# Two graph layers on one core: layer 1's values and residual taken from rows by VectorE instead of from transposes by TensorE and ScalarE

## The chip, the cores and the metric

The kernel runs on one core of a Trainium2 chip. A core has TensorE (matrix products, written to PSUM), VectorE and ScalarE (elementwise work on PSUM and SBUF), GpSimd, and DMA queues. The metric is the device time of one execution in microseconds, the median of several runs. The profile is of one execution.

## The reference

The input is x (16 batches of 1024 rows of 256 numbers, float32) and adj (16 x 1024 x 1024, zeros and ones, about 3% ones).

Layer 0 is graph attention with 4 heads of 64. With one edge type present its logit is a source term plus a destination term, through a leaky ReLU, masked by adj:

```
h = einsum('bnd,hde->bhne', x, W)
weight = leaky_relu(mask * (e_src[i] + e_dst[j]), 0.01)      # -1e9 where adj is 0
out = relu(softmax(weight) @ h + bias) + h
out = (out - mean) / sqrt(var + 1e-6) * ln_gamma + ln_beta   # over the 64 of each head
x = layernorm(x + heads side by side)                        # over 256
```

Layer 1 is attention with 8 heads of 32, in which queries, keys and values are one and the same tensor, and then an MLP:

```
normed = layer_norm(x, gamma1, beta1)
out = softmax(normed @ normed.T / sqrt(32), masked by adj) @ normed
x1 = x + out
y = layer_norm(x1, gamma2, beta2)
mlp = gelu(y @ W1 + b1) @ W2 + b2                            # 256 -> 1024 -> 256
x = layernorm(x + x1 + mlp)
```

All products are float32.

## The kernel before

**Tiles.** A batch's 1024 rows are 8 blocks of 128; four blocks make a half of 512. Two streams of steps, `layer0` and `layer1`, run over the batches; layer 0 of the next batch is interleaved with layer 1 of the present one. All instructions are issued through one recording helper, so the profile gives every one the line L61 and groups are told apart by tile names.

**Layer 0** (`prepare`, line 471; `attention0`, 541). A batch's rows are turned (`xT`), multiplied with the weights (`acc<-w0e,xT`), and the adjacency rows are turned by TensorE and made into a mask by ScalarE (`mask`). The softmax weights of layer 0 are made by VectorE (`p<-cb,dinv,mask`), and 16 steps per batch multiply them with the values (`acc<-v,p`). When one head of one half is done, `residual0` (line 616) takes the reciprocal of the sums, divides and applies ReLU, and adds the result to `hb`. Before the change the middle part is four ScalarE activations, one for each block of 128 rows, scaled by that row's reciprocal. `after0` (626) then norms each head, adds the input, takes the statistics of the 256, and makes

- `normed` (tile `sq`): the rows after both norms, which ScalarE computes from `hb`;
- `nT`: these rows turned by TensorE (`transpose_rows`, 376), with gamma1 and beta1 applied by ScalarE as it copies them from PSUM, where they are numbers per partition. These are layer 1's queries and keys;
- `v1` (tile `v`): the values, with a column of ones. Before the change `nT` is turned back by TensorE, eight 128x128 transposes for a half, into two PSUM tiles, and copied by ScalarE;
- `x1`: the residual, `normed` times a ratio per row, by ScalarE. `ratio` undoes the second norm's scale.

**Layer 1** (`attention1`, 710). 32 steps per batch. A step makes logits for four heads (`ps<-nT`, four PSUM tiles), exponentials by ScalarE (`p<-ps`), the mask by VectorE (`p<-p,mask`), and, three steps later (`LAG`), the weighted products (`po<-p,v`, `po<-p,unit`, `po<-v,p`). `finish1` (816) adds x1, norms and turns; it also adds the attention result to x1, and `add_bias2` (837) adds the row b2. The MLP (`mlp`, 848) has TensorE groups `ps<-yT,w_sb` and `po<-w_sb,hid` with ScalarE's gelu between; `last_norm` (907) adds x1, norms and writes a block out (tile `z`).

**PSUM.** Two banks `acc` serve layer 0 and the transposes while layer 1 is in its attention (`bank0`, 357); a bank is taken when the chain that reads it has been issued. While the MLP runs, transposes use the four `ps` banks (`side_bank`, 370). So the turning back of `nT` shows as `acc<-ident,nT` and as `ps<-ident,nT`.

**What sets the order.** Each engine runs its instructions in the order of the program, and the program is written by a planner. `Pace` (line 90) keeps a modelled time for each engine: `enter` (143) gives each instruction a start and an end from modelled costs. `chains` holds the side work (residuals, norms, transposes) as generators; each `yield` names the engine of what follows and the tiles that it needs, and `advance` (433) lets those go on whose needs are met in the model. The main loop (line 997) takes the next step from `layer0` or `layer1` by comparing layer 0's progress with a wanted course: `COURSE` (982) says how far layer 0 is to be when layer 1 has done so much of its batch. The model's times exist only while the program is written; on the chip the engines wait for each other by semaphores.

Of the kernel before, what the change touches and what calls it, by code (L numbers as in the profile page):

```python
# [31 lines left out]
F32 = mybir.dt.float32  # L32
# [4 lines left out]
OP = mybir.AluOpType  # L37
PSUM = bass.MemoryType.PSUM

P = 128  # L40
# [49 lines left out]
class Pace:  # L90
# [5 lines left out]
    def __init__(self, nc):  # L96
        self.nc = nc
        self.free = dict.fromkeys(self.LATENCY, 0.0)
        self.written, self.read = {}, {}
        self.array = self.table = self.last = None  # L100

        self.born = self.settle = lambda tile: None
        for name in self.LATENCY:
            setattr(self, name, Engine(self, name))
# [38 lines left out]
    def enter(self, engine, op, args, kwargs):  # L143
        aps = [a for a in (*args, *kwargs.values()) if isinstance(a, bass.AP)]
        out, ins = aps[0].tensor.name, [a.tensor.name for a in aps[1:]]
        if op == "dma_start":
            start = max(self.now(), self.through(out))
            self.written[out] = start + self.LATENCY["sync"]
            return
        start = max(  # L150
            [self.free[engine], self.read.get(out, 0.0)] + [self.written.get(i, 0.0) for i in ins if i != out]
        )
        end = self.free[engine] = start + self.cost(engine, op, aps, args[2] if len(args) > 2 else None)
        self.written[out] = max(self.written.get(out, 0.0), end + self.LATENCY[engine])
        if "accum_out" in kwargs:
            out = kwargs["accum_out"].tensor.name
            self.written[out] = max(self.written.get(out, 0.0), end + self.LATENCY[engine])
        for i in ins:
            self.read[i] = max(self.read.get(i, 0.0), end)
# [3 lines left out]
def fast_path(  # L163
# [120 lines left out]
    for i, (_, _, dst) in enumerate(terms):  # L284
# [8 lines left out]
                )  # L293
            nc.vector.tensor_reduce(dst[:, c, :], t, axis=mybir.AxisListType.X, op=OP.add)

    lng0_r, lnb0_r, b2_r = [
        const.tile([P, D], F32, name=name) for name in ("lng0_r", "lnb0_r", "b2_r")
    ]
    g1_c, be1_c, g2_c, be2_c = [const.tile([P, DC], F32, name=name) for name in ("g1_c", "be1_c", "g2_c", "be2_c")]
    w1_sb = const.tile([P, DC, DFF], F32, name="w1_sb")  # L300
# [3 lines left out]
    def at_time(t):  # L304
        return lambda: t

    def later_weights():
        for t, src in ((lng0_r, lng0), (lnb0_r, lnb0), (b2_r, b2)):
            nc.sync.dma_start(t, bass.AP(tensor=src.tensor, offset=src.offset, ap=[[0, P], [1, D]]))
        for t, src in ((g1_c, gamma1), (be1_c, beta1), (g2_c, gamma2), (be2_c, beta2)):  # L310
            nc.sync.dma_start(t, src.rearrange("(c p) -> p c", p=P))
        nc.sync.dma_start(b1_sb, b1.rearrange("c p -> p c"))
        yield "tensor", at_time(nc.now() + 6.0)
        nc.sync.dma_start(w1_sb, w1.rearrange("(c p) f -> p c f", p=P))
        nc.sync.dma_start(w2_sb, w2.rearrange("(c p) d -> p c d", p=P))
        yield "tensor", at_time(nc.now() + 24.0)

        pb = ps_o.tile([P, FC], F32, name="po")
        for f in range(FC):
            for c in range(DC):  # L320
                nc.tensor.matmul(
                    pb[:, f : f + 1],
                    w1_sb[:, c, f * P : (f + 1) * P],
                    be2_c[:, c : c + 1],
                    start=c == 0,
                    stop=c == DC - 1,
                )
        yield "vector", pb
        nc.vector.tensor_add(b1_sb, b1_sb, pb)
        for c in range(DC):  # L330
            nc.vector.tensor_scalar(w1_sb[:, c, :], w1_sb[:, c, :], g2_c[:, c : c + 1], None, op0=OP.mult)
# [283 lines left out]

    def residual0(av, h, rinv):

        t = two.tile([P, BPH, HO], F32, name="relu")
        nc.vector.reciprocal(rinv, av[:, :, HO])
        yield "scalar", rinv  # L620
        for q in range(BPH):
            nc.scalar.activation(t[:, q, :], av[:, q, 0:HO], AF.Relu, scale=rinv[:, q : q + 1])
        yield "vector", t
        nc.vector.tensor_add(h, h, t)

    def after0(b, n, hd, o):


        for first in range(hd + 1):
            complete(residuals[b, n, first])  # L630
        rowwise = [P, BPH, D]
        heads = slice((hd - PAIR + 1) * HO, (hd + 1) * HO)
        oh = o[:, :, heads].rearrange("p g (h e) -> p g h e", e=HO)
        per_head = [P, BPH, PAIR, HO]
        s = small.tile([P, BPH, PAIR], F32, name="s0")
        nc.vector.tensor_reduce(s, oh, axis=mybir.AxisListType.X, op=OP.add)
        nc.vector.scalar_tensor_tensor(
            oh, s[:, :, :, None].to_broadcast(per_head), -1.0 / HO, oh, op0=OP.mult, op1=OP.add
        )
        yield "scalar", o  # L640
        sq = two.tile([P, BPH, PAIR * HO], F32, name="oT1")
        nc.scalar.activation(sq, o[:, :, heads], AF.Square)
        if hd == H0 - 1:
            xl = one.tile(rowwise, F32, name="xl")
            load_x(xl, b, n * BPH, BPH)
        yield "vector", sq
        v = small.tile([P, BPH, PAIR], F32, name="v0s")
        nc.vector.tensor_reduce(
            v, sq.rearrange("p g (h e) -> p g h e", e=HO), axis=mybir.AxisListType.X, op=OP.add
        )  # L650
        nc.vector.tensor_scalar(v, v, 1.0 / HO, EPS_HEAD, op0=OP.mult, op1=OP.add)
        r = power(v.rearrange("p g e -> p (g e)"), BPH * PAIR, "r0").rearrange("p (g e) -> p g e", e=PAIR)
        pair = o[:, :, heads]
        nc.vector.tensor_mul(pair, pair, lng0_r[:, None, heads].to_broadcast([P, BPH, PAIR * HO]))
        if hd == H0 - 1:
            nc.vector.tensor_add(xl, xl, lnb0_r[:, None, :].to_broadcast(rowwise))
        yield "vector", r
        nc.vector.tensor_mul(oh, oh, r[:, :, :, None].to_broadcast(per_head))
        if hd < H0 - 1:
            return  # L660
        complete(norms[b, n, PAIR - 1])
        nc.vector.tensor_add(o, o, xl)
        yield "vector", o
        mv = small.tile([P, BPH, 2], F32, name="mv0")
        for g in range(BPH):
            statistics(o[:, g, :], mv[:, g, :])

        v2 = small.tile([P, 2, BPH], F32, name="v2")  # L670
        nc.vector.tensor_scalar(v2[:, 0, :], mv[:, :, 1], 1.0 + EPS, EPS * EPS, op0=OP.mult, op1=OP.add)
        r2 = power(v2[:, 0, :], BPH, "r2")
        nc.vector.tensor_scalar(v2[:, 1, :], mv[:, :, 1], EPS, None, op0=OP.add)
        r3 = power(v2[:, 1, :], BPH, "r3")
        yield "vector", r2
        t = minus_mean(mv[:, :, 0], r2, BPH)
        yield "scalar", t
        normed = one.tile(rowwise, F32, name="sq")
        scale_shift(normed, o, t, r2, BPH)
        yield "tensor", normed, side_ready  # L680
        nT = two.tile([P, DC, HALF], F32, name="nT")
        for g in range(0, BPH, GB):
            transpose_rows(nT[:, :, g * P : (g + GB) * P], normed[:, g : g + GB, :], g1_c, be1_c)
            yield "tensor", normed, side_ready
        yield "tensor", nT, side_ready
        v1 = two.tile([P, BPH, H1, HD + 1], F32, name="v1")
        nc.vector.memset(v1[:, :, :, HD], 1.0)
        for g in range(0, BPH, GB):
            pt = side_bank([P, GB, DC, P])
            for i in range(GB):  # L690
                for c in range(DC):
                    nc.tensor.transpose(pt[:, i, c, :], nT[:, c, (g + i) * P : (g + i + 1) * P], ident)
            nc.scalar.copy(
                v1[:, g : g + GB, :, 0:HD], pt.rearrange("p g c (h e) -> p g (c h) e", e=HD)
            )
            yield "tensor", nT, side_ready
        handed[b, n] = [None, v1, nT]
        yield "vector", r3

        ratio = small.tile([P, BPH], F32, name="ratio")  # L700
        nc.vector.tensor_mul(ratio, v2[:, 0, :], r2)
        nc.vector.tensor_mul(ratio, ratio, r3)
        yield "scalar", ratio
        x1 = three.tile(rowwise, F32, name="x1")
        for g in range(BPH):
            nc.scalar.mul(x1[:, g, :], normed[:, g, :], ratio[:, g : g + 1])
        handed[b, n][0] = x1


# [195 lines left out]
            yield 1.75, before_ready  # L905

    def last_norm(b, k, po, x1):
        z = four.tile([P, 1, D], F32, name="z")
        nc.vector.tensor_add(z[:, 0, :], po, x1)
        mv = small.tile([P, 2], F32, name="mv")  # L910
        statistics(z[:, 0, :], mv)
# [67 lines left out]
    ATTN1 = 2.0 + 2.5 * (NH * NB * H1 // QUAD)  # L979
    WORK1 = ATTN1 + NB // GB * (1.75 * FC / 2 + 3.5 * GB)  # L980
    SLACK = 0.06
    COURSE = [(0.0, 1.0), (ATTN1, 1.40), (WORK1 - 10.0, 2.0), (WORK1, 2.0)]

    def wanted():
        b, done = place[1]
# [475 lines left out]
```

## Time and profile before

| | before |
|---|---|
| time, median of 3 (lowest to highest) | 3663.35 us (3662.82 to 3672.89) |
| span of the profiled execution | 3665.6 us |
| mean granted TensorE clock | 0.976 |
| TensorE busy | 3506.3 us |
| VectorE busy | 2840.2 us |
| ScalarE busy | 2191.5 us |
| GpSimd busy | 428.7 us |

From the second batch on, a batch repeats after 223.8 to 223.9 us. A row of the groups gives engine and operation, output tile and inputs, their shapes, the count, then the busy time of the group and the mean length of one instruction in ns, then the idle time of that engine in front of them and what ended it. A row of the waits gives the engine and the tile it was about to write, the engine and tile it waited for, the total in us, how often, and the longest.

### The profile page before, as it was taken

To read this page: it belongs to the slowest core of one execution; us is meant where nothing else is said; L and a number is where in the kernel's file an instruction comes from. 1 tells how busy PE (TensorE), PEld (TensorE's weight loads), DVE (VectorE), ACT (ScalarE), POOL (GpSimd) and SP (SyncE) were. 2 spreads that over 40 slices of the span, in tenths; PEclk is the share of its full clock that TensorE was granted. 3 is DMA by queue.
4 is the path that set the end of the run, shared out by engine and by line. 5 is a ranking of instruction groups with operands and counts; after the bars stand their busy time and mean duration, and the time that the engine had idled before them with its cause. 6 is when DMAs were issued, how large, how long until landed. Compare 5 with 4: busy or idle time off the path is not lost.

```text
span 3665.6 us, 142190 instructions
## 1 busy us (share of the span) xinstructions
PE 3506.3 (96%) x64673; PEld 2368.4 (65%) x64673; DVE 2840.2 (77%) x4882; ACT 2191.5 (60%) x5024; POOL 428.7 (12%) x424
## 2 busy tenths in 40 slices
PE   6899999999999999999999999999999999999998
PEld 4567575675856658576585766757567585665846
DVE  5787787878878787787887868778787887878784
ACT  2665746557475574746647466574755747557474
POOL 0102011010110101101020110201101011010100
PEclk9899999999999999999999999999999999999999
DMA  4111101011010110201101011110101102010000
GB/s 102 33 18 33 29 14 37 15 37 24 15 41 11 36 23 16 45 6 40 20 27 34 13 35 17 33 29 14 39 14 35 26 14 43 11 36 9 16 6 14
DMA packets 77525, 97.30 MB, mean 27 GB/s; under 512 B 9072, under 2 KB 59760, under 8 KB 76912
## 3 DMA queue, kind: packets, MB, share of 16 engines
q0 software_dynamic: 18432, 33.56, 6.1%
q1 hardware_dynamic: 56896, 53.50, 4.6%
q8 instruction: 508, 8.32, 0.9%
q10 hardware_dynamic: 1584, 1.05, 0.1%
q14 instruction: 105, 0.86, 0.1%
HBM read 104.87 MB, written 16.78 MB: 33 GB/s over the span
## 4 chain that ended last, share of the span: by engine, by line
PE 87%; ACT 8%; DVE 3%; issue 1%; DMA 0%; ACTq 0%; POOL 0%; POOLq 0%; DVEq 0%
PE ps L61 33%; PE po L61 33%; PE acc L61 21%; ACT p L61 3%; DVE p L61 2%; ACT mask L61 1%; ACT sq L61 1%; ACT nT L61 1%; ACT v L61 0%; ACT relu L61 0%; DMA w0e<-in_L_gnn_W_dram 0%; ACT z L61 0%; ACT cb L61 0%; DVE z L61 0%; ACT oT L61 0%
## 5 line engine op out<-in xcount | busy, mean ns | idle before, releaser
L61 ACT ACTIVATE p<-ps 128x512 f32<-128x512 f32 x2048 | 1061.8, 617 | 402.1 <-PE ps L61 402.1
L61 DVE TENSOR_TENSOR p<-p,mask 128x1024 f32<-128x1024 f32 x1024 | 1187.9, 1218 | 103.0 <-ACT p L61 101.3
L61 PE MATMUL ps<-nT 32*128 32x512 f32 x4096 | 795.4, 654 | 11.0 <-ACT cb L61 9.8
L61 DVE SCALAR_TENSOR_TENSOR p<-cb,dinv,mask 128x512 f32<-128x512 f32 x1024 | 698.9, 744 | 28.6 <-ACT cb L61 28.6
L61 PEld LDWEIGHTS po<-v,p 128*32 128x32 f32 x32768 | 401.1, 111 | 323.5 <-issue 279.7
L61 PE MATMUL acc<-v,p 128*64 128x65 f32 x16384 | 546.2, 225 | 28.6 <-ACT relu L61 13.2
L61 PEld LDWEIGHTS acc<-v,p 128*64 128x64 f32 x16384 | 507.4, 139 | 96.1 <-issue 47.4
L61 PE MATMUL po<-p,v 128*32 128x512 f32 x2048 | 559.1, 621 | 0.0
L61 PE MATMUL po<-p,unit 128*32 128x512 f32 x2048 | 558.5, 621 | 0.0
L61 ACT ACTIVATE hid<-ps,b_sb 128x256 f32<-128x256 f32 x512 | 241.4, 476 | 437.1 <-PE ps L61 435.0
L61 PE MATMUL ps<-yT,w_sb 128*128 128x256 f32 x2048 | 480.0, 384 | 0.0
L61 PE MATMUL po<-w_sb,hid 128*128 128x256 f32 x2048 | 477.0, 384 | 0.0
L61 PEld LDWEIGHTS po<-w_sb,hid 128*128 128x128 f32 x2048 | 382.4, 190 | 74.5 <-issue 22.7
L61 PEld LDWEIGHTS ps<-yT,w_sb 128*128 128x128 f32 x2048 | 379.8, 190 | 51.8
L61 PE MATMUL po<-v,p 128*32 128x33 f32 x32768 | 392.5, 199 | 4.6 <-issue 4.5
L61 PEld LDWEIGHTS ps<-nT 32*128 32x128 f32 x4096 | 284.9, 187 | 153.2 <-ACT p L61 52.0
L61 PEld LDWEIGHTS po<-p,v 128*32 128x32 f32 x2048 | 79.4, 109 | 339.9 <-DVE p L61 171.9
L61 POOL TENSOR_TENSOR r<-v,mhalf 128x1 f32<-128x1 f32 (+1 forms) x192 | 168.0, 880 | 574.7 <-DVE v L61 540.1
L61 DVE TENSOR_TENSOR z<-acc,bias_r 128x256 f32<-128x256 f32 x128 | 54.2, 423 | 219.5 <-ACT hb L61 217.8
L61 POOL TENSOR_TENSOR r<-v1s,mhalf 128x4 f32<-128x4 f32 x32 | 61.9, 1934 | 1214.9 <-DVE v1s L61 1214.9
L61 POOL TENSOR_TENSOR r<-v0s,mhalf 128x8 f32<-128x8 f32 x64 | 128.9, 2014 | 522.6 <-DVE v0s L61 522.6
L61 POOL DMA_DIRECT2D ak<-in_adj_dram x128 | 69.8, 545 | 914.3 <-PE acc L61 903.9
(113 smaller groups left out, 3078.8 us busy)
## 6 DMA issues: line engine op xcount, KB each, us to landing
ak<-in_adj_dram POOLq DMA_DIRECT2D x128, 256.0 KB, 4.0
xk<-in_x_dram SPq DMA_DIRECT2D x64, 256.0 KB, 3.4
xl<-in_x_dram SPq DMA_DIRECT2D x32, 512.0 KB, 4.0
out_dram<-z SPq DMA_DIRECT2D x128, 128.0 KB, 1.7
w_sb<-in_L_gnn_W_dram SPq DMA_DIRECT2D x2, 1024.0 KB, 6.6
v<-in_L_gnn_a_src_dram SPq DMA_DIRECT2D x2, 320.0 KB, 4.9
v<-in_L_gnn_a_dst_dram ACTq DMA_DIRECT2D x1, 320.0 KB, 7.0
xl<-in_L_gnn_a_dst_dram ACTq DMA_DIRECT2D x1, 320.0 KB, 6.2
```

Of the source, the lines that this page charges most:

```text
L61: return method(*args, **kwargs)
```

## The change

Layer 1's values are `normed` times gamma1 as a row, computed by VectorE, so that nothing is turned back. Beta1 is left out of the values: the attention weights of a row sum to one, so that it adds beta1 to every output, and it goes into x1 instead, which VectorE makes in one instruction (times ratio, plus the row). Because x1 is added twice on the way to the output, b2 is made b2 - beta1 once at the start. ReLU and division of layer 0 become one VectorE product per head and half, max(av, 0) times the reciprocal. In the planner, TensorE's costs are doubled for a while behind a modelled wait of over 1.5 us[...]; the course's middle point goes from 1.40 to 1.42. The ReLU tile has one buffer instead of two, and `z` three instead of four, which makes room for two rows of constants.

```diff
@@ Pace.enter
-        end = self.free[engine] = start + self.cost(engine, op, aps, args[2] if len(args) > 2 else None)
+        cost = self.cost(engine, op, aps, args[2] if len(args) > 2 else None)
+        if engine == "tensor":
+            if start > self.free[engine] + 1.5:
+                self.slow = start + 3.0
+            if start < self.slow:
+                cost *= 2.0
+        end = self.free[engine] = start + cost
@@ later_weights
-        for t, src in ((lng0_r, lng0), (lnb0_r, lnb0), (b2_r, b2)):
+        for t, src in ((lng0_r, lng0), (lnb0_r, lnb0), (g1_r, gamma1), (be1_r, beta1), (b2_r, b2)):
...
+        nc.vector.tensor_sub(b2_r, b2_r, be1_r)
@@ residual0
-        t = two.tile([P, BPH, HO], F32, name="relu")
+        t = one.tile([P, BPH, HO], F32, name="relu")
         nc.vector.reciprocal(rinv, av[:, :, HO])
-        yield "scalar", rinv
-        for q in range(BPH):
-            nc.scalar.activation(t[:, q, :], av[:, q, 0:HO], AF.Relu, scale=rinv[:, q : q + 1])
-        yield "vector", t
+        nc.vector.scalar_tensor_tensor(
+            t, av[:, :, 0:HO], 0.0, rinv[:, :, None].to_broadcast([P, BPH, HO]), op0=OP.max, op1=OP.mult
+        )
         nc.vector.tensor_add(h, h, t)
+        yield from ()
@@ after0
-        yield "tensor", nT, side_ready
+        yield "vector", normed
         v1 = two.tile([P, BPH, H1, HD + 1], F32, name="v1")
         nc.vector.memset(v1[:, :, :, HD], 1.0)
-        for g in range(0, BPH, GB):
-            pt = side_bank([P, GB, DC, P])
-            for i in range(GB):
-                for c in range(DC):
-                    nc.tensor.transpose(pt[:, i, c, :], nT[:, c, (g + i) * P : (g + i + 1) * P], ident)
-            nc.scalar.copy(
-                v1[:, g : g + GB, :, 0:HD], pt.rearrange("p g c (h e) -> p g (c h) e", e=HD)
+        for g in range(BPH):
+            nc.vector.tensor_mul(
+                v1[:, g, :, 0:HD],
+                normed[:, g, :].rearrange("p (h e) -> p h e", e=HD),
+                g1_r.rearrange("p (h e) -> p h e", e=HD),
             )
-            yield "tensor", nT, side_ready
...
-        yield "scalar", ratio
+        yield "vector", ratio, at_time(nc.now() + 12.0)
+
         x1 = three.tile(rowwise, F32, name="x1")
         for g in range(BPH):
-            nc.scalar.mul(x1[:, g, :], normed[:, g, :], ratio[:, g : g + 1])
+            nc.vector.scalar_tensor_tensor(
+                x1[:, g, :], normed[:, g, :], ratio[:, g : g + 1], be1_r, op0=OP.mult, op1=OP.add
+            )
@@ last_norm
-        z = four.tile([P, 1, D], F32, name="z")
+        z = three.tile([P, 1, D], F32, name="z")
@@ the course
-    COURSE = [(0.0, 1.0), (ATTN1, 1.40), (WORK1 - 10.0, 2.0), (WORK1, 2.0)]
+    COURSE = [(0.0, 1.0), (ATTN1, 1.42), (WORK1 - 10.0, 2.0), (WORK1, 2.0)]
```

More of the change, by code (lines that the diff above doesn't have):

```diff
@@ L100, in __init__ @@
         self.array = self.table = self.last = None
+        self.slow = 0.0
         self.born = self.settle = lambda tile: None
@@ L294, in fast_path @@
             nc.vector.tensor_reduce(dst[:, c, :], t, axis=mybir.AxisListType.X, op=OP.add)
-    lng0_r, lnb0_r, b2_r = [
-        const.tile([P, D], F32, name=name) for name in ("lng0_r", "lnb0_r", "b2_r")
+    lng0_r, lnb0_r, g1_r, be1_r, b2_r = [
+        const.tile([P, D], F32, name=name) for name in ("lng0_r", "lnb0_r", "g1_r", "be1_r", "b2_r")
     ]
```

## The prediction

> **What bounds the kernel now.** I read the page first (busy shares, slices, chain), then TensorE's own waits over the whole run, then the groups that the diff touches, and last the timeline of one handover between batches.
>
> ```profile
> PE 3506.3 (96%) x64673; PEld 2368.4 (65%) x64673; DVE 2840.2 (77%) x4882; ACT 2191.5 (60%) x5024; POOL 428.7 (12%) x424
> ...
> PE   6899999999999999999999999999999999999998
> ...
> PE 87%; ACT 8%; DVE 3%; issue 1%; DMA 0%; ACTq 0%; POOL 0%; POOLq 0%; DVEq 0%
> ```
>
> TensorE is busy for 96% of the span and makes 87% of the chain that ended last. VectorE has 3665.6 - 2840.2 = 825 us free, ScalarE 1474 us. So taking work off TensorE, or a wait in front of it, shortens the run; moving work from ScalarE to VectorE costs nothing as long as VectorE keeps up in each stage. TensorE's waits over the run:
>
> ```profile
> PE acc L61 <- ACT mask L61: 37.3, 34, 9.7
> PE acc L61 <- ACT nT L61: 18.7, 19, 1.1
> PE acc L61 <- ACT relu L61: 14.5, 17, 1.4
> ...
> PE acc L61 <- ACT v L61: 10.7, 15, 0.7
> ```
>
> Columns: total us, times, longest. Three of these four come about once per batch (17 to 19, 17 and 15 times for 16 batches), and they wait for tiles that the change makes elsewhere. The groups:
>
> ```profile
> L61 PE MATMUL acc<-ident,nT 128*128 128x128 f32 x136 | 24.6, 333 | 18.3 <-ACT nT L61 17.6 <-ACT v L61 0.7
> L61 PE MATMUL ps<-ident,nT 128*128 128x128 f32 x120 | 15.5, 273 | 0.0
> L61 ACT ACTIVATE relu<-acc,ranges 128x64 f32<-128x64 f32 x512 | 118.2, 319 | 31.5 <-DVE ranges L61 30.1
> L61 ACT ACTIVATE x<-sq,ratio 128x256 f32<-128x256 f32 x128 | 54.6, 501 | 28.3 <-DVE ratio L61 28.3
> L61 DVE TENSOR_TENSOR hb<-hb,relu 128x256 f32<-128x256 f32 x128 | 54.2, 424 | 156.4 <-ACT relu L61 156.4
> L61 DVE TENSOR_TENSOR o<-acc,ranges 128x256 f32<-128x256 f32 x48 | 20.4, 425 | 1.7
> L61 DVE SCALAR_TENSOR_TENSOR hb<-s,hb 128x512 f32<-128x512 f32 x64 | 44.3, 692 | 2.2
> ```
>
> The first two rows are the 256 transposes back from nT, 40.1 us of TensorE; one form waits 18.3 us in front. The fifth shows VectorE idle 156.4 us for ScalarE's ReLU. The last two price what is added. Then the chain in one handover (1915 to 1940 us, the ninth):
>
> ```profile
> 1930.74 2.75 PE po L61 x72
> 1933.49 0.60 PE acc L61 x4
> 1934.09 0.02 issue
> 1934.11 1.03 ACT nT L61 x2
> 1935.14 0.04 issue
> 1935.19 0.67 PE acc L61 x4
> 1935.86 0.02 issue
> 1935.88 0.46 ACT v L61
> 1936.34 0.02 issue
> 1936.36 0.60 ACT v L61
> 1936.96 0.04 issue
> 1937.01 0.87 PE acc L61 x6
> ```
>
> After the last four transposes of `normed` (end 1934.09) TensorE waits for nT, turns it back, and waits for the values' copy, because the next work in its order needs that PSUM bank. From 1934.09 to 1937.01 is 2.92 us per batch in which the chain holds nothing but the step that is deleted.
>
> [...] in the handover the granted clock is 0.84 and 0.81 in two 10 us windows, and four transposes take 1.11 us at 1926.73 against 0.66 us at 1933.42. [...]
>
> **The change, part by part.**
>
> *Values from the rows.* Removed: 256 transposes and 64 ScalarE copies. One half of each batch lies in the MLP stretch, where TensorE is solid: there its eight transposes take 1.04 us and hold the next matmul off for 1.0 to 1.2 (weights from 1890.37, next product 1891.55); I take 1.1. The other half lies in the handover: 2.92. Sum 4.0 per batch, x16 = 64 us. In the new order a weighted product follows the last transposes there, then the fifth logit step; the product needs weights of three steps earlier and values of the first half, both long ready, and hides nT's 1.03 us evacuation. Added: 128 VectorE products of 256, 0.425 each = 54 us (1.7 per half). They wait for ScalarE's `normed`, and in front of VectorE's queue that wait blocks the masks behind it. In the handover the masks are consumed three steps later, a step being 2.63 us of TensorE (1792.92 to 1795.55) against 2.35 us of masks, so 1.7 us fit.
>
> *ReLU as one product per head.* Removed: 512 activations (118.2 us of ScalarE), a hop to ScalarE's queue and back, and so the 14.5 us (0.9 per batch) in which TensorE waits for the bank that ReLU still reads: the bank is now released by VectorE right behind its reciprocal. Added: 128 products from PSUM, 0.425 each = 54 us. VectorE's idle time for ReLU (156.4 us) is three times that, so it comes nearly free. The path that ends a batch loses 1905.09 to 1907.88 (reciprocal to addition, 2.8 us) for about 0.6, but ScalarE's queue decides the handover (the rows of `sq`, `mask` and `p`), so I count nothing for it.
>
> *x1.* 128 activations (54.6 us) leave ScalarE; 128 scalar_tensor_tensor enter VectorE. No row has this shape: from 692 ns at 512 with 1.03 ns an element ((1218-424)/768) it is 0.43; from the 744 ns of the masked maximum, which has a per-partition scalar too, 0.477. I take 0.45: 58 us. Its reader, the residual after attention, comes a quarter of a batch later or more.
>
> *The rest.* Two row loads and one subtraction of 256 elements, once (0.4 us, beside the first batch). Beta leaves the values and comes back as a row in x1, at no instruction. `z` with three buffers: each use takes the buffer of the third before it, at the tightest place 18.2 us back (uses at 1897.88, 1902.99, 1913.00, 1916.12), and that block left ScalarE for its write at 1902.83. `relu` with one buffer is written and read by VectorE alone. These cost nothing.
>
> *The order.* Doubled TensorE cost after a modelled wait and 1.42 for 1.40 move work between the streams. In the handover the sequence up to the fourth logit step, on ScalarE too, is what it was, so its half-clock stretch stays. After it the mask and projection steps stand apart, each between logit steps, where before two or three stood together. That may take some of the 37.3 us of waits for masks, or cost others; I put it at nothing, +-15 us.
>
> *Sum.* 64 + 14.5 = 78.5 us off the path. The same counted otherwise: 40.1 busy + 18.7 + 14.5 + 10.7 of waits = 84. Against it: VectorE gets 54+54+58 = 166 us, 10.4 per batch, on 176.7 of a batch's 223.85. Where it is near full (9.7 and 9.8 of 10 us in 1989.7 to 2009.7; 9.9 in the first batch's attention, where layer 0 runs alone) the excess shows. The first batch takes 8 ReLU products (3.4 us) there; elsewhere I put 0.8 us per batch, 12 us. In all 15 us back: 3663.35 - 78.5 + 15 = 3600.
>
> **Rivals.**
>
> *A: only the transposes' own time is won.* New waits of TensorE, for VectorE's masks or bank releases, replace the 44 us of waits: 3663 - 40 = 3623. For: the projection's bank already waits for VectorE (13.1 us over 37 times), and VectorE's queue gets longer. Against: in the attention stretch after a handover VectorE had 2 to 3.5 us in 10 free.
>
> *B: the half-clock stretch goes too.* Some 7 us at half clock per handover ((0.16+0.19) x 10 x 2), worth 3.5 us, x15 = 52: 3548. For: the residual chain gets shorter. Against: the same ScalarE work stands before it.
>
> *C, slower: VectorE becomes the bound.* If all 10.4 us per batch land on the path: 166 - 78.5 = +88, 3751; if half do, 3668. For: 97% of VectorE in two windows of that batch. Against: 3006 us is 83% of 3600, and the products that would have to be exposed stand where it idles for ReLU or had room.
>
> **How the numbers follow.** Forecast 3600: 0.60. A: 0.22. B: 0.08. C: 0.06, a part of it at no change. The rest, a reordering that loses 30 to 60 us somewhere that I have not seen: 0.04. The range: down to 3570 (84 us and 10 from the order), up to 3634 (A and 11 us from the order); that leaves out B, C and the last, 18 in 100. Over 0.3% faster is below 3652: 0.92; within 0.3%: 0.04; slower: 0.04.
>
> **What would show it.** The transposes of nT gone; matmul busy near 3466; TensorE's waits for relu and for the values zero, for nT near zero; after the handover's last `sq` transposes a weighted product without a gap; batches 219 to 220 us apart for 223.85; VectorE near 3000, ScalarE near 1983 us; the 0.81 to 0.84 windows still there. A TensorE wait for masked weights (`p`) or for `z` grown by over 20 us would prove A; VectorE above 95% over whole batches, C.

## The result and the profile after

The changed kernel takes 3573.26 us (median of four, 3564.78 to 3577.13) where the kernel before takes 3663.09 us beside it: ratio 0.9746, 95% interval 0.9721 to 0.977. That is 90 us less; 63 were forecast. From the page of the changed kernel, busy shares and the chain that ended last:

```profile
PE 3443.4 (97%) x64417; PEld 2329.2 (65%) x64417; DVE 2989.8 (84%) x5267; ACT 2010.2 (56%) x4320; POOL 413.7 (12%) x424
...
PE 91%; ACT 5%; DVE 2%; issue 1%; DMA 0%; POOL 0%; ACTq 0%; POOLq 0%; DVEq 0%
```

TensorE is busy 63 us less, and ScalarE and VectorE have lost shares of the chain: 5% and 2% for 8% and 3%. TensorE's waits, those that the prediction named:

```profile
PE acc L61 <- ACT mask L61: 22.6, 17, 1.4
...
PE ps L61 <- ACT nT L61: 1.1, 1, 1.1
PE acc L61 <- ACT nT L61: 1.1, 1, 1.1
```

There is no row left for `relu` or for the values. nT has fallen from 18.7 to 2.2 us, and the waits for masks by 15 us; 9.7 us of these were a single wait near the start, and the changed kernel has one of 10.4 us at that place too, only put down to another cause. One wait is new: 13.1 us, once, for `sq` at the end of the first batch's layer 0. The new VectorE groups:

```profile
L61 DVE SCALAR_TENSOR_TENSOR relu<-acc,ranges 128x256 f32<-128x256 f32 x128 | 54.3, 425 | 4.4
L61 DVE SCALAR_TENSOR_TENSOR x<-sq,ratio,be_r 128x256 f32<-128x256 f32 x128 | 53.3, 477 | 0.1
L61 DVE TENSOR_TENSOR v<-sq,g_r 128x256 f32<-128x256 f32 x128 | 44.9, 410 | 0.9 <-ACT sq L61 0.7
```

The fourth field is the busy time and the length of one: 425, 477 and 410 ns, where 425, 450 and 425 were taken. The 0.7 us in the last row is all that VectorE's queue stood for ScalarE's `normed`. The chain of one handover, the stretch in which layer 1's attention of a batch begins while the last rows of the batch's second half are made, to be held against that of the kernel before in the prediction:

```profile
1651.37 1.96 ACT sq L61 x4
1653.33 1.10 ACT mask L61 x2
1654.43 0.04 issue
1654.48 0.66 PE acc L61 x4
1655.13 3.23 PE ps L61 x6
1658.36 1.05 PE acc L61 x4
1659.41 2.75 PE po L61 x72
1662.15 1.71 PE ps L61 x8
```

The first two rows are ScalarE's, which makes the rows of `sq` and then masks. The row at 1658.36 is the second group of `sq` transposes. The weighted product (`po`) follows at once, and the 2.92 us of copies and transposes are gone. But the rows from 1655.13 to 1662.15 are slow: 72 products in 2.75 us, as before. The granted clock, the share of its full clock that TensorE is given, says why. The windows of this handover, first of the kernel before, then of the changed one (columns: stretch, its length, busy time of TensorE, its weight loads, VectorE, ScalarE and GpSimd, granted clock, DMA share, GB/s):

```profile
1924.40:1931.40 7.00, 5.57 (x20) 2.73 (x23) 4.67 (x7) 7.00 (x19) 0.00 (x0) 0.66 0.38 77
1931.40:1938.40 7.00, 5.16 (x98) 3.39 (x90) 3.38 (x6) 4.08 (x10) 0.00 (x0) 0.86 0.01 2
```

```profile
1651.70:1658.70 7.00, 5.38 (x18) 2.75 (x19) 4.63 (x7) 7.00 (x19) 0.00 (x0) 0.85 0.37 76
1658.70:1665.70 7.00, 7.00 (x159) 3.46 (x160) 5.86 (x12) 3.71 (x9) 0.00 (x0) 0.66 0.01 2
```

Both handovers have a half-clock stretch of 7 us that begins in a window in which ScalarE is busy 7.00 of 7.00 us. In the kernel before TensorE then idles 1.8 us more. Half clock is a granted clock of 0.5; the traces of these two kernels show no value but 0.5 and 1.

**An account per batch.** The table splits each run's batch. The period runs from one start of layer 1's attention to the next, taken at ScalarE's table loads, as a mean of the 14 batches from the second on. (In the kernel before single periods run from 222.2 to 226.2 us; the 223.8 to 223.9 us given ahead of the prediction are near the mean and not the spread.) Idle is the time in it without a matmul. Half clock is 2 x (1 - granted clock) x length, summed over 40 windows of each batch. What is left takes off the idle time and half of the half-clock time, an estimate, since TensorE does not work through all of that time.

"Half normed" is the version in which VectorE makes the `sq` rows of each batch's second half, and dead transposes are made but not used; all versions are described below.

| run | time us | ratio to before (95%) | period | idle | half clock | left |
|---|---|---|---|---|---|---|
| before | 3663 to 3667 | | 224.0 | 6.3 | 9.0 | 213.2 |
| changed | 3573.3 | 0.9746 (0.9721 to 0.9770) | 217.1 | 2.9 | 5.6 | 211.4 |
| rows alone | 3571.0 | 0.9743 (0.9729 to 0.9757) | 217.6 | 4.8 | 4.6 | 210.5 |
| ReLU alone | 3674.8 | 1.0021 (1.0011 to 1.0030) | 224.4 | 8.1 | 7.6 | 212.5 |
| planner alone | 3633.9 | 0.9913 (0.9899 to 0.9926) | 221.5 | 4.3 | 5.9 | 214.2 |
| changed, old planner | 3577.8 | 0.9754 (0.9742 to 0.9767) | 218.3 | 3.7 | 6.8 | 211.1 |
| changed, dead transposes | 3604.4 | 0.9828 (0.9807 to 0.9849) | 219.5 | 3.2 | 6.3 | 213.1 |
| changed, ReLU on ScalarE | 3569.1 | 0.9736 (0.9715 to 0.9757) | 217.4 | 4.2 | 5.9 | 210.2 |
| half normed on VectorE | 3521.3 | 0.9600 (0.9578 to 0.9622) | 213.7 | 2.3 | 1.5 | 210.6 |
| all normed on VectorE | 3521.5 | 0.9599 (0.9579 to 0.9619) | 213.8 | 2.4 | 1.7 | 210.6 |
| half normed, ReLU on ScalarE | 3577.9 | 0.9754 (0.9738 to 0.9770) | 217.5 | 5.0 | 5.1 | 210.0 |
| half normed, old planner | 3531.9 | 0.9637 (0.9620 to 0.9653) | 215.1 | 3.0 | 2.9 | 210.6 |
| before, half normed | 3599.2 | 0.9808 (0.9793 to 0.9824) | 219.2 | 4.9 | 2.0 | 213.3 |
| half normed, blocks on VectorE | 3546.7 | 0.9667 (0.9650 to 0.9684) | 215.4 | 3.8 | 3.9 | 209.7 |

The last column is the check on the account: 212.5 to 214.2 in the five kernels that have the transposes, 209.7 to 211.4 in the nine that have not. So two causes, idle time and half clock, and the transposes between them hold all fourteen runs to about 1 us a batch. Period, idle and half clock are of one execution. In that of the changed kernel, its fastest, three of the 14 handovers had no half clock, and its mean clock is 0.983; its other three runs have 0.978 to 0.979, so that their half clock must be some 2 us a batch more than the 5.6 (an estimate: twice the difference in clock, times 3573 us, over 15 batches).

### The profile page after: what moved, and what is told of

Same layout as the page of the kernel before. It is cut to its first block, busy times and chain, and to the rows that moved or that the text cites. A ratio compares the mean times of both kernels' runs of the same rounds, so it can differ in the third digit from the quotient of the medians.

```text
span 3563.0 us, 141472 instructions
## 1 busy us (share of the span) xinstructions
PE 3443.4 (97%) x64417; PEld 2329.2 (65%) x64417; DVE 2989.8 (84%) x5267; ACT 2010.2 (56%) x4320; POOL 413.7 (12%) x424
## 4 chain that ended last, share of the span: by engine, by line
PE 91%; ACT 5%; DVE 2%; issue 1%; DMA 0%; POOL 0%; ACTq 0%; POOLq 0%; DVEq 0%
PE po L61 36%; PE ps L61 34%; PE acc L61 21%; ACT p L61 2%; DVE p L61 1%; ACT sq L61 1%; ACT mask L61 1%; ACT xT L61 0%; ACT z L61 0%; DMA w0e<-in_L_gnn_W_dram 0%; DVE hb L61 0%; ACT cb L61 0%; ACT hb L61 0%; POOL r L61 0%; DVE z L61 0%
## 5 line engine op out<-in xcount | busy, mean ns | idle before, releaser
L61 POOL TENSOR_TENSOR r<-v,mhalf 128x1 f32<-128x1 f32 (+1 forms) x192 | 152.8, 801 | 842.0 <-DVE v L61 493.0
L61 PE MATMUL acc<-w0e,xT 128*128 128x264 f32 x512 | 149.3, 415 | 20.0 <-issue 10.4
```

Source lines behind the costliest of these rows:

```text
L61: return method(*args, **kwargs)
```

## The experiments

**Rows alone: the kernel before with the values and x1 from the rows.** The edits of `later_weights`, v1, ratio and x1 are those of the change; ReLU and the planner are as before. The two new rows of constants take the place of two buffers of the output block's tile.

```diff
-        z = four.tile([P, 1, D], F32, name="z")
+        z = two.tile([P, 1, D], F32, name="zz")
...
```

> The kernel before with the values and x1 alone changed: both made from the rows by VectorE, beta in the residual; ReLU stays on ScalarE, the planner as before; the output block's tile has two buffers. Theory 1 (the prediction's sum: the transposes and the waits they bring are the bulk): 64 us off and about 8 back for VectorE, so 3607, between 3600 and 3615; TensorE's waits for the values gone and for nT near zero, its wait for relu still near 14 us. Theory 2 (the order is the bulk of what came beyond the forecast): the same here, but then run e3 alone gains 25 us or more. Theory 3 (VectorE takes back half): 3635 or more.

3571 us, which is 95 off; none of the three theories. The rows do by themselves all that the whole change does. Per batch the last column falls by 2.7, the transposes' part, idle time by 1.5, and half clock from 9.0 to 4.6 us, worth 2.2. TensorE's waits for the values and nT went as expected, and the wait for `relu` stayed (16.8 us).

**ReLU alone: the kernel before with one VectorE product per head.**

```diff
-        for q in range(BPH):
-            nc.scalar.activation(t[:, q, :], av[:, q, 0:HO], AF.Relu, scale=rinv[:, q : q + 1])
+        nc.vector.scalar_tensor_tensor(
+            t, av[:, :, 0:HO], 0.0, rinv[:, :, None].to_broadcast([P, BPH, HO]), op0=OP.max, op1=OP.mult
+        )
```

> The kernel before with ReLU and division alone changed to one VectorE product per head. Theory 1: 14.5 us of TensorE waits off and 4 to 6 back in the first batch, so 3649 to 3655. Theory 2 (the shorter chain from the last head to the rows brings the next batch's logits forward): 3640 or less, with a shorter half-clock stretch at the handover. Theory 3 (VectorE full): 3663 or more.

3674.8: slower, by 0.1 to 0.3%, the side of theory 3, though VectorE is only 79% busy over the run. TensorE's longest waits in this run (`z` here and below is the values' tile `z<-acc,bias_r`, which VectorE makes from layer 0's projection and so frees its bank, not the output block of the same name):

```profile
PE acc L61 <- ACT oT L61: 47.2, 31, 2.6
PE acc L61 <- DVE z L61: 42.0, 37, 2.9
PE acc L61 <- ACT nT L61: 23.5, 31, 1.1
```

The 14.5 us for `relu` are down to 1.8, and others took their place, in an order that the planner made anew: oT had 10.6 us before, `z` 13.1, nT 18.7. Idle time rose by 1.8 us a batch.

**Planner alone: the kernel before with half clock behind modelled waits, and 1.42.** No instruction is added or removed. The 1.5 and 3.0 us in it are the planner's own numbers, which no run tested; the factor of 2 is the granted clock of 0.5.

```diff
+            if start > self.free[engine] + 1.5:
+                self.slow = start + 3.0
+            if start < self.slow:
+                cost *= 2.0
...
-    COURSE = [(0.0, 1.0), (ATTN1, 1.40), (WORK1 - 10.0, 2.0), (WORK1, 2.0)]
+    COURSE = [(0.0, 1.0), (ATTN1, 1.42), (WORK1 - 10.0, 2.0), (WORK1, 2.0)]
```

> The kernel before with the planner alone changed: half clock behind modelled waits, and the course's 1.42. No instruction is added or removed. Theory 1 (the order at nothing, plus or minus 15): 3650 to 3678. Theory 2 (the order is what brought 25 us beyond the forecast): 3640 or less, with TensorE's waits for masks well under 37 us.

3633.9, theory 2: 32 us from the order alone, 2.0 us less idle time and 3.1 us less half clock per batch.

**The changed kernel with the old planner.** The same lines taken out again.

> The changed kernel with the planner of before: no half clock behind waits, course 1.40. Theory 1: 3573 to 3588, since the order is worth 15 at most. Theory 2: 3598 to 3603, the forecast that took the order at nothing, with more waits for masks than the changed kernel's 22.6 us and a batch period of 219 us.

3577.8, theory 1's side: on top of rows and ReLU the planner is worth 4 us, which is not clear of nothing (ratios 0.9754 and 0.9746, intervals that overlap). So the parts do not add: rows 95, planner 32, ReLU -9 make 118, and together they give 90. Each of planner and rows by itself takes idle time and half clock away, so they seem to take away the same thing. From rows alone to this run ReLU does remove idle time (4.8 to 3.7), as forecast, but half clock rises from 4.6 to 6.8, and the first MLP stretch starts at 264.0 instead of 257.6 us. Part of that is the execution: the profile has a mean clock of 0.977, the run with the median time 0.979.

**The transposes put back, their results unused.** The changed kernel, with the 256 transposes of nT in their old places; nobody copies their PSUM tiles, and the values come from the rows.

```diff
+        yield "tensor", nT, side_ready
+        for g in range(0, BPH, GB):
+            pt = side_bank([P, GB, DC, P])
+            for i in range(GB):
+                for c in range(DC):
+                    nc.tensor.transpose(pt[:, i, c, :], nT[:, c, (g + i) * P : (g + i + 1) * P], ident)
+            yield "tensor", nT, side_ready
         yield "vector", normed
```

> The changed kernel with the 256 transposes of nT put back in their places, their PSUM tiles taken but never copied: the values still come from the rows, so the transposes' results are unused. This prices the transposes and the PSUM banks they take without the wait for ScalarE's copy. TensorE's order at the handover is then one weighted product, the transposes, and on. Theory 1 (the sum of the prediction): the transposes' own time, 1.1 us in each half, so 35 us more than the changed kernel: 3600 to 3612; half-clock time per batch as in the changed kernel (5.6 us). Theory 2 (the transposes bring the handover's half-clock stretch with them): 3625 or more, with half-clock time back at 8 us or more per batch.

3604.4, theory 1: 31 us for 256 transposes, about 0.12 us each. Half clock stays near the changed kernel's (6.3 for 5.6; the runs' median clock is 0.979 with them and 0.978 to 0.979 without). So transposes that wait for nothing do not bring it. What remains of the rows' 95 us is not the transposes' own time; it must come from the waits around them or from the order, and these two were not told apart.

**The changed kernel with ReLU back on ScalarE.** The inverse of the second experiment's diff; the output block's tile has two buffers instead of three, to make room.

> The changed kernel with ReLU and division back on ScalarE (the output block's tile has two buffers): values, x1 and the planner stay changed. Theory 1 (ReLU is worth its 14.5 us of waits): 3583 to 3590. Theory 2 (ReLU on VectorE is worth nothing beside the other two, as its run alone was slower than before): 3560 to 3576. Theory 3 (the gains of the parts add, so that rows and order without ReLU give the best): about 3571 - 32 = 3540.

3569.1, theory 2: beside rows and planner, ReLU on VectorE gains nothing in this kernel (ratios 0.9736 and 0.9746, intervals that overlap). And the parts do not add, so theory 3 falls.

**Normed rows of the handover on VectorE.** ScalarE is busy 7.00 of 7.00 us ahead of the half-clock stretch, and its four activations for `sq` hold 1.96 us of the chain there. This run moves them for the second half of each batch; TensorE's order is the changed kernel's, instruction for instruction (the two traces differ in 17 of 64417 places, all among products that start within 1 us of each other).

```diff
-        yield "scalar", t
         normed = one.tile(rowwise, F32, name="sq")
-        scale_shift(normed, o, t, r2, BPH)
+        if n == 0:
+            yield "scalar", t
+            scale_shift(normed, o, t, r2, BPH)
+        for g in range(BPH if n else 0):
+            nc.vector.tensor_scalar(
+                normed[:, g, :], o[:, g, :], r2[:, g : g + 1], t[:, g : g + 1], op0=OP.mult, op1=OP.add
+            )
```

> The changed kernel with the normed rows of the second half of each batch, the half of the handover, made by four VectorE products instead of four ScalarE activations; TensorE's order is the same, instruction for instruction. Theory A (the handover waits for ScalarE, and the half clock follows from that wait): ScalarE's 2.0 us of these rows leave the chain, half-clock time per batch falls from 5.6 us to 3.5 or less, 2.5 to 4 us per batch: 3515 to 3540. Theory B (the handover is set by TensorE or VectorE): within 8 us of the changed kernel, 3565 to 3581, or slower if the four products in front of the masks delay the projection's bank.

3521.3, theory A. Half clock falls from 5.6 to 1.5 us a batch, and in 8 of 14 handovers there is none. The two windows of one of them:

```profile
1851.10:1858.10 7.00, 6.18 (x100) 3.51 (x100) 6.93 (x12) 6.99 (x18) 0.00 (x0) 1.00 0.41 79
1858.10:1865.10 7.00, 7.00 (x179) 3.23 (x179) 6.90 (x11) 5.06 (x10) 0.00 (x0) 1.00 0.01 2
```

With a shorter wait and at full clock TensorE gets 100 matmuls into the first of them, where the changed kernel's gets 18. It is the fastest version of the study, 3.8 to 4.2% below the kernel before.

**The same for both halves** (without the condition on n).

> The changed kernel with the normed rows of both halves made by VectorE. The first half's lie in the MLP stretch, where TensorE was solid. Theory A and B as for the second half alone; for the first half both expect nothing: within 6 us of that run. If VectorE's load in the MLP stretch is near its limit, 5 to 15 us slower than that run.

3521.5: nothing more, as both expected. In the MLP stretch TensorE was not waiting for ScalarE.

**Half normed, ReLU on ScalarE.** The sixth and the seventh run's edits together.

> The run with the second half's normed rows on VectorE, with ReLU and division back on ScalarE and two buffers for the output block's tile. Theory 1 (ReLU on VectorE only pays in half-clock time or the first batch what it saves in waits; with the half clock nearly gone its saved waits remain): 3530 to 3540, slower than 3521. Theory 2 (ReLU on VectorE is worth nothing or less in any case): 3505 to 3522.

3577.9: neither; it loses 57 us, all that had been won. VectorE's rows in one handover, first with ReLU on VectorE, then on ScalarE:

```profile
1847.88 1.38 DVE L61 TENSOR_SCALAR sq<-hb,r,t 128x256 f32<-128x256 f32 x4
1849.18 2.35 DVE L61 TENSOR_TENSOR p<-p,mask 128x1024 f32<-128x1024 f32 x2
1851.45 0.41 DVE L61 TENSOR_TENSOR z<-acc,bias_r 128x256 f32<-128x256 f32 x1
```

```profile
1880.26 1.38 DVE L61 TENSOR_SCALAR sq<-hb,r,t 128x256 f32<-128x256 f32 x4
1881.56 2.35 DVE L61 TENSOR_TENSOR p<-p,mask 128x1024 f32<-128x1024 f32 x2
1883.82 0.42 DVE L61 TENSOR_TENSOR z<-acc,bias_r 128x256 f32<-128x256 f32 x1
```

The next batch's first logits start at 1842.62 and 1873.29, so `sq` begins 5.3 us after them in the first run and 7.0 us in the second: the chain from the last head is longer by ScalarE's ReLU. On VectorE the masks and then `z`, which frees the projection's bank, stand behind it without a gap, and TensorE, whose order in this stretch is the same in both runs, waits for `z` 0.89 us in the first case and 2.60 us in the second:

```profile
1851.92 1.16 PE L61 MATMUL acc<-w0e,xT 128*128 128x264 f32 x4 [0.89 <-DVE z L61]
```

```profile
1884.30 2.13 PE L61 MATMUL acc<-w0e,xT 128*128 128x264 f32 x4 [2.60 <-DVE z L61]
```

Over the runs:

```profile
PE acc L61 <- DVE z L61: 16.7, 21, 0.9
```

```profile
PE acc L61 <- DVE z L61: 40.7, 22, 2.6
PE acc L61 <- ACT relu L61: 17.7, 17, 4.6
```

With the extra 24 us of waiting comes half clock in all 14 handovers of the second run, 5.1 us a batch for 1.5, and the waits for `relu` are back as well. So once ScalarE is out of the way VectorE's queue sets the handover, and there ReLU on VectorE is worth 57 us, by the shorter residual chain and by the waits for `relu` together.

**Half normed, old planner.** The seventh run without the planner's change.

> The run with the second half's normed rows on VectorE, with the planner of before (no half clock behind waits, course 1.40). Theory 1 (the planner's gain of 32 us without the rows was only the half-clock stretch, which is nearly gone here): within 8 us of 3521. Theory 2 (the order is worth something by itself, fewer waits for masks): 3530 to 3555.

3531.9: theory 2, at its near edge. The new planner is worth about 11 us here, 0.7 us of idle time and 1.4 us of half clock per batch.

**The kernel before, half normed on VectorE.** The seventh run's edit on the kernel before, nothing else. There, too, ScalarE's rows stand in the chain of the handover:

```profile
1923.63 1.96 ACT sq L61 x4
1925.58 1.10 ACT mask L61 x2
```

> The kernel before with one thing changed: the second half's normed rows made by VectorE. Theory 1 (the handover of the kernel before waits for ScalarE too, and its 9 us of half clock per batch follow from that): half-clock time down to 3 us or less per batch, 3.0 us for it and 1.4 us of waits for masks, so 60 to 70 us off: 3595 to 3605. Theory 2 (the kernel before is held at the handover by the transposes and their copies too, so that freeing ScalarE alone leaves the half clock): 3625 to 3650.

3599.2, theory 1: 68 us from moving 64 instructions, half clock from 9.0 to 2.0, with all transposes still in the kernel. So the kernel before too was held there by ScalarE. But TensorE's order was not quite held in this run: behind the transposes of nT the planner put a logit step and a weighted product ahead of the next block's transposes, which in the kernel before wait 0.7 us a handover for the values' copy, and that wait is gone. How much of the 68 us is the new order's was not tested.

**Half normed, and the output blocks' last scaling on VectorE.**

```diff
-        yield "scalar", t
-        scale_shift(z, z, t, r, 1)
+        nc.vector.tensor_scalar(z[:, 0, :], z[:, 0, :], r, t, op0=OP.mult, op1=OP.add)
```

> The run with the second half's normed rows on VectorE, with the output blocks' last scaling on VectorE too, 128 products. Two of these stand in the handover on ScalarE, 1.3 us. Theory 1 (the handover still waits for ScalarE): 3495 to 3512. Theory 2 (what is left there waits for VectorE, as the 16.7 us of waits for the projection's bank say): 3515 to 3535.

3546.7, slower than either theory said: TensorE's wait for `z` rises to 36.9 us and half clock to 3.9. That fits VectorE's queue as the one that was left to wait for.

## Why the prediction was right or wrong

The measured 3573 us lie inside the stated range of 3570 to 3634 us, near its lower end, 27 us below the forecast of 3600. The main mechanism, work and waits taken off TensorE by the values from the rows, was right; the terms of the sum were not all right, and that the total came out this near is in part luck: ReLU's 14.5 us that were not won and VectorE's 15 us that were not lost cancel.

- **TensorE bounds, and work off it shortens the run: right.** The 256 transposes alone are 31 us when put back.
- **Values from the rows, 64 us: right in kind, too small.** The waits for nT and the values are gone. Rows alone brought 95 us. By the table 2.7 us a batch of it are the transposes and 1.5 idle time, over 15 batches 63 us, as the sum had it; the other 2.2 a batch, 33 us, are half clock, which the sum did not contain.
- **ReLU, 14.5 us: wrong.** Its waits went (from 14.5 us to none), but the time did not: alone it costs 9 us, beside rows and planner it gains nothing. The step counted a wait removed as time won, though the planner wrote a new order in which other waits stood. Where it does pay, the term that was set at nothing has a part in it, the shorter chain from the last head, and only once ScalarE no longer decides the handover.
- **The half-clock stretch stays: wrong, and this is the term that was mis-sized.** It was argued from the unchanged sequence ahead of it. It begins as before, behind a wait for a mask that is 1.44 us in most handovers of both kernels, but on the mean it is shorter, and TensorE no longer idles behind it: 5.6 for 9.0 us a batch. In the kernel before five of 14 handovers had 13.7 us of it, in the changed one the longest has 10.2. Half of 3.4 us over 15 batches is 25 us in the profiled execution, which lies 35 us below the forecast. By the mean clocks, 0.976 before and 0.978 to 0.979 in the other three runs, half clock is worth 9 to 13 us of the 27 by which the median was off (an estimate: 0.024 x 3663 less 0.021 or 0.022 x 3573). So this is rival B, 52 us, for half of its size in the profiled execution and for a quarter or less by the median.
- **The order at nothing, plus or minus 15: right in this kernel**, 4 us and not clear of nothing, and wrong alone, 32.
- **VectorE takes 15 us back: not seen.** Its load came as forecast (2989.8 us for 3006), idle time fell all the same. The first batch does not settle it: its MLP stretch starts 3.5 us earlier (257.65 for 261.11 us), but this execution had 10 us less half clock up to the second batch's attention (27.3 for 37.5), which by the account is worth 5 us.
- **Rivals A and C: fell.** No wait that comes in every batch took the place of the 44 us; the one of 13.1 us for `sq` comes once, and the planner alone brings one of 8.3 us there. VectorE is at 84%.

That the waits around the transposes are what kept the clock down longer fits the runs with dead transposes and with rows alone. It was not isolated, since each kernel's order is planned anew; the run that isolates a cause with TensorE's order held is that of the normed rows.

## What to carry to other kernels

Where a trace shows TensorE's clock halved behind a stall, as here for 1.5 to 9.0 us a batch, price the stall as the wait plus half of the slow time, an estimate that held fourteen runs here to about 1 us a batch, and look at which engine is full just ahead of it: moving one small group off that engine gave 52 us here with TensorE's order held, and 68 us where the order changed too, more than the transposes themselves. Judge by the clocks of several executions, since one can be lucky. Parts of a change that remove the same stall do not add, so test them singly and together. A wait that disappears from the list is not yet time won if a planner writes the order anew.

## What the runs showed of the hardware that was not expected

The clock fell to half behind short waits. In the handover of the changed kernel shown above TensorE's longest wait is 1.44 us, in the half normed run it is 0.89 us and in that run with ReLU on ScalarE 2.60 us. TensorE's work around these waits is thin as well: ahead of the 1.44 us eight logit products take 2.53 us, where eight take 1.14 us at the start of the handover. No run separates the wait from the thin work.

Where a handover falls in time also decides. In the traces of the kernel before and of the changed one all changes of the clock lie whole multiples of 3.41 us apart, as marks on one ruler; in the eight runs from the dead transposes on, the granted clocks of the windows fit such a ruler to 0.07 us. So half-clock time per batch comes in steps: 0, 3.4, 6.8, 10.2 and 13.7 us. In the half normed run the wait is the same in all 14 handovers, 0.88 to 0.90 us at the same place. The clock fell in the six in which a mark lies between 0.4 us before and 0.8 us after the end of that wait, and it stayed full in the other eight, whose next mark comes 1.0 to 2.6 us after it. So handovers that are alike in the program lose different times, and so do runs of one kernel: 3564.78 us at a mean clock of 0.983, 3571.71 to 3577.13 at 0.978 to 0.979.
